# A four-layer-norm attention and feed-forward block: finer first loads, one values step moved ahead of the scores, and a gate on GpSimd's side work

## The chip, the cores and the metric

The kernel runs on one core of a Trainium2 chip. A core has five engines that work side by side, each with its own queue of instructions: TensorE (PE in the profile, with its weight loads as PEld), VectorE (DVE), ScalarE (ACT), GpSimd (POOL) and SyncE (SP), which here only issues DMAs. DMAs are issued from the queues of SP, ACT and POOL. The metric is the device time of one execution in microseconds; the number of a version is the median of its runs.

## The reference

For x of shape 4 x 1024 x 256 (batch, tokens, width), all in float32, the block computes an attention with 16 heads of 16 columns, and a feed-forward with ternary weights, each between two layer norms and with a residual:

```python
def _L0_attn_ref(x, Wqkv, Wout):
    qkv = (x @ Wqkv.T).reshape(B, S, 3, H, Dh)
    qkv = jnp.transpose(qkv, (2, 0, 3, 1, 4))
    q, k, v = (qkv[0], qkv[1], qkv[2])
    scores = jnp.einsum('bhqd,bhkd->bhqk', q, k) * scale
    attn = _stable_softmax(scores)
    out = jnp.einsum('bhqk,bhkd->bhqd', attn, v)
    out = jnp.transpose(out, (0, 2, 1, 3)).reshape(B, S, D)
    return out @ Wout.T
...
h = jax.nn.silu(_tlin(h, w1_w, w1_s)) * _tlin(h, w2_w, w2_s)
h = jax.nn.gelu(_tlin(h, h1_w, h1_s), approximate=False)
h = jax.nn.gelu(_tlin(h, h2_w, h2_s), approximate=False)
return _tlin(h, w3_w, w3_s)
...
x = x + _layernorm(_L0_attn_ref(_layernorm(x, axis=-1), L0_attn_Wqkv, L0_attn_Wout), axis=-1)
x = x + _layernorm(_L0_ffn_ref(_layernorm(x, axis=-1), L0_ffn_w1_w, ...), axis=-1)
```

## The kernel before, in words

**Attention** runs first, for all four batches (b), and takes the first 574 us. It is cut into units: one unit is one batch, one group g of four heads (there are four groups) and one half h of 512 queries. A unit has eight steps c over 128 keys each, and each step has two tiles (u), so 32 units make 512 tiles. For each tile, `exponentials` (lines 547 to 555) multiplies k and q into a score tile `s` of 128 x 1024 in PSUM, and ScalarE writes its exponential into a ring of eight tiles, `e`. `weigh` (557) multiplies the exponentials with the values, which lie in `vaug`, and sums them into the one accumulator `acc`. `rise` (567) keeps a running maximum `top` of the exponentials on VectorE; a ring tile may be written again only when `weigh` and `rise` have read it. `unit_end` (821) transposes the finished accumulator on VectorE (line 824, `o<-acc`), which frees it for the next unit.

The scores are computed from high and low parts of q and k, which must lie in a special order in the tiles `sk` and `sq`. `copies` and `stack` (491 to 526) bring them there by 32 DMA copies for each group (line 500), issued in steps of six: four on SP's queue and two on GpSimd's. Groups 0 and 1 take them from one set of projections, groups 2 and 3 from a second. `slots` (528) copies the values of a group into `vaug` (line 532), on GpSimd except for group 0 of batch 0.

**The main loop** (1464 to 1501) writes the order of all instructions by hand. One round of it makes three score tiles, weighs about as many, and calls `side.take`. `Side` (715) holds chains of `Step`s: a step runs when its `gap` of rounds since the step before it has passed, when `ready()` says so, when TensorE is free of another side step in the round if it needs TensorE, and when its estimated `work` fits. Side chains hold the projections, values and norms of the next batch (`prologue`, 347; `begin`, 789), the ending of the last one (`ending`, 644), the copies of the next stack, and the weight work. The variable `weighed` counts the tiles weighed so far, so `tiles[weighed][3]` is the step c of the unit that is at hand.

**The weight work** on GpSimd prepares the feed-forward's weights. `round_weights` (279) loads a block of `w1`, `w2` or `w3` (line 288), rounds it (292) and stores it (293); six blocks. `round_corners` (299) loads a corner of `h1` or `h2` by two DMAs (309), rounds three quarters of it in two casts (319, 320) and stores them, and then makes four sums and differences (327 to 330) and stores those (312); sixteen corners. The loaded block `w` and the result `wr` have one buffer each, so the sums wait until the store before them has landed. GpSimd also computes the reciprocal roots of all norms (line 107, `rstd`).

**The start** has its own order (1407 to 1454). `load_x(0, [0])` loads x's first 512 tokens on SP's queue, tile 0 by one DMA and tiles 1 to 3 by another (`pieces`, 166), since the halves of the tokens are interleaved; then come the two halves of wqk, with x's second 512 tokens between them. Eight warm-up products on zeros (1413, `idle`) keep TensorE busy meanwhile. VectorE takes statistics of the tiles (97, 98), GpSimd their root, VectorE normalises (140, `xn`), TensorE transposes (381, `pt`), ScalarE copies (342, `xT`), TensorE projects q and k (339, `p`), and the 64 copies of the first stack go out on three queues. Then two of four values steps (`values`, 386; 339, `pv`) run, and the first slots are filled (1448). `alone = False` ends the phase in which side work may use the score tiles' PSUM and ScalarE. The two remaining values steps (1451) are side steps of the first rounds.

**The feed-forward** follows from 574 us on. The change does not touch its code.

Of the kernel before, what the change touches and what calls it, by code (L numbers as in the profile page):

```python
# [73 lines left out]
class Step:  # L74


    def __init__(self, run, gap=0, tensor=True, heavy=False, work=0, split=False):
        self.run, self.gap, self.tensor, self.heavy, self.work, self.split = run, gap, tensor, heavy, work, split
        self.ready = lambda: True


class Norms:
# [61 lines left out]
def tile_fast(ctx: ExitStack, tc: tile.TileContext, x, wqk, wv, wo, w1, w1s, w2, w2s, h1, h1s, h2, h2s, w3, w3s, out, bad):  # L144
    nc = tc.nc
    B, S, D = x.shape
# [3 lines left out]
    NT = S // P  # L150
# [15 lines left out]
    def pieces(h, view):  # L166

        t, n = NH + (TPQ - 1) * h, TPQ * h
        return (slice(n, n + 1), view[:, h : h + 1, :]), (slice(n + 1, n + TPQ), view[:, t : t + TPQ - 1, :])

    def load_x(b, halves=range(NH)):
        view = x[b].rearrange("(t p) d -> p t d", p=P)
        for h in halves:
            for at, tokens in pieces(h, view):
                n = at.stop - at.start
                m = 1 if b == B - 1 else n
                for k in range(0, n, m):
                    nc.sync.dma_start(out=xs[b][:, at.start + k : at.start + k + m, :], in_=tokens[:, k : k + m, :])


    ctx.enter_context(tc.manual_schedule())
    load_x(0, [0])
    ident = const.tile([P, P], F32, name="ident")
    make_identity(nc, ident)
# [28 lines left out]
    with ExitStack() as actx, ExitStack() as rctx:  # L213
# [60 lines left out]
        work = actx.enter_context(tc.tile_pool(name="work", bufs=2, side="right"))  # L274

        def misc(name):
            return ps_misc.tile([P, NQ], F32, tag="misc", name=name)

        def round_weights(n, c):

            st = {}

            def rows(w):
                return w[c * P : (c + rows_at_once[n]) * P, :].rearrange("(i p) d -> p i d", p=P)

            def load():
                st["w"] = work.tile([P, WIDE], F32, tag="w", name="w", bufs=1)
                nc.gpsimd.dma_start(out=st["w"].rearrange("p (i d) -> p i d", i=rows_at_once[n]), in_=rows(weights[n]))

            def cast():  # L290
                st["r"] = work.tile([P, WIDE], F32R, tag="wr", name="wr", bufs=1)
                nc.gpsimd.tensor_copy(st["r"], st["w"])
                nc.gpsimd.dma_start(out=rows(rounded[n]).bitcast(F32), in_=st["r"].bitcast(F32).rearrange("p (i d) -> p i d", i=rows_at_once[n]))

            return [Step(load, 2, False), Step(cast, 4, False)]

        made_factors = [0]

        def round_corners(n, c, x):


            st = {}
            half = NQ // 2

            def load():
                st["w"] = work.tile([P, WIDE], F32, tag="w", name="w", bufs=1)
                rows = weights[n].rearrange("(j c p) (i x n) -> c x p j i n", j=2, p=P, i=2, x=2)[c, x]
                for j in range(2):
                    nc.gpsimd.dma_start(out=st["w"].rearrange("p (j i n) -> p j i n", j=2, i=2)[:, j], in_=rows[:, j])

            def store(r, k0, k1):
                nc.gpsimd.dma_start(
                    out=factors[n][k0:k1, :, c, x * half : (x + 1) * half].rearrange("k p n -> p k n").bitcast(F32),
                    in_=r.bitcast(F32).rearrange("p (k n) -> p k n", n=half)[:, : k1 - k0],
                )

            def plain():
                r = work.tile([P, WIDE], F32R, tag="wr", name="wr", bufs=1)
                nc.gpsimd.tensor_copy(r[:, 0:half], st["w"][:, 0:half])
                nc.gpsimd.tensor_copy(r[:, half : 3 * half], st["w"][:, 2 * half : 4 * half])  # L320
                store(r, 0, 3)

            def sums():
                r = work.tile([P, WIDE], F32R, tag="wr", name="wr", bufs=1)
                s1, s2, s3, s4 = (r[:, k * half : (k + 1) * half] for k in range(4))
                a11, a21, a12, a22 = (st["w"][:, k * half : (k + 1) * half] for k in range(4))
                nc.gpsimd.tensor_tensor(s1, a21, a22, ALU.add)
                nc.gpsimd.tensor_tensor(s2, s1.bitcast(F32), a11, ALU.subtract)
                nc.gpsimd.tensor_tensor(s3, a11, a21, ALU.subtract)
                nc.gpsimd.tensor_tensor(s4, a12, s2.bitcast(F32), ALU.subtract)  # L330
                store(r, 3, 7)
                made_factors[0] += 1

            return [Step(load, 2, False), Step(plain, 3, False), Step(sums, 1, False)]

        def by_slots(o, w, i, **flags):

# [190 lines left out]
        def slots(b, g, t0=0, t1=NT, engine=nc.gpsimd):  # L528


            def run():
                engine.tensor_copy(
                    vaug[g % 2][:, t0:t1, :, 0:DH], cv[:, t0:t1, HPG * DH * g : HPG * DH * (g + 1)].rearrange("p t (h e) -> p t h e", e=DH)
                )
                slotted[g % 2] = b, g, t1

            return run
# [3 lines left out]
        tiles = [(b, g, h, c, u) for b in range(B) for g in range(NG) for h in range(NH) for c in range(NT) for u in range(2)]  # L541
# [173 lines left out]
        class Side:  # L715


            def __init__(self):
                self.first, self.rest, self.slot = [], [], 0
                self.room, self.open, self.tired = 0.0, None, False  # L720
# [58 lines left out]
        side = Side()  # L779
        accs, tops, ends, later = {}, {}, {}, {"qk": 0, "qk1": None}  # L780

        def add_flags(steps):

            if later.setdefault("flags", [[]])[0]:
                later["flags"][0].extend(steps)
            else:
                later["flags"] = side.add(steps)
# [33 lines left out]
        def unit_end(b, g, h):  # L821

            o = both.tile([P, NQ], F32, tag="o", name="o", bufs=2)
            nc.vector.transpose(o, accs[b, g, h])  # L824
            unit = side.add((divide_last if (b, g) == (B - 1, NG - 1) else divide)(g, h, o, tops[b, g, h]), True)
            if b and not g:

                unit[0][-1].ready = lambda: not any(step.tensor for step in ends[b - 1, h][0])
            if g == NG - 1:
                last = ending(b, h, to_scalar if (b, h) == (B - 1, NH - 1) else to_vector)  # L830
                unit[0].extend(last)
                ends[b, h] = unit
            if h < NH - 1:
                return

            n, at = g + 2, b
            if n >= NG:
                n, at = n - NG, b + 1
            if b == B - 1 and g == NG - 2:
                side.add([Step(lambda q=q: load_factor(q), 2 if q else 0, False) for q in range(SLOTS // 2)])  # L840
            if at < B:
                put = Step(slots(at, n), 0, False)
                if at > b:
                    later["chain"][0].append(put)
                else:
                    put.run()
                side.add(stack(at, n))
            if g == NG - 3 and b + 1 < B:
                later["chain"][0].extend(later["rest"])
            elif g == NG - 3:  # L850
                chunks = [(n, [c]) for n in ("w1", "w2") for c in range(DC)]
                loads = [Step(lambda n=n, c=c: load_weights(n, c), 2 if n == "w1" else 1, False) for n, c in chunks]

                loads[0].ready = lambda: not later["flags"][0]
                loads[DC].ready = lambda: not outstanding
                side.add(loads)
                second = prepare(1, to_vector)
                second[-DC].ready = lambda: not outstanding
                side.add([Step(lambda: None, 3, False)] + prepare(0, to_vector) + second)
            if g == NG - 1:  # L860
                begin(b + 1)
# [545 lines left out]
        norm, xt, qk, v, flags = prologue(0, first_space, first_copy)  # L1407
# [39 lines left out]
            step.run()  # L1447
        slots(0, 0, 0, NT // 2, nc.vector)()
        alone = False
        load_x(1)  # L1450
        side.add(v[2:] + [Step(slots(0, 0, NT // 2, NT, nc.vector), 0, False), Step(slots(0, 1), 0, False)] + sum(qk[1], []) + [Step(lambda: later.update(qk1=0, v=0), 0, False), Step(lambda: add_flags(flags[0] + flags[1]), 0, False)])
        begin(0)
        side.add(stack(0, 1) + few(load_rest(), 1))
        side.add([s for k in blocks for s in round_weights(*k)] + [s for k in corners for s in round_corners(*k)])
# [9 lines left out]
        while weighed < len(tiles):  # L1464
            n = end = made
# [3 lines left out]
            if made == len(tiles):  # L1469
                n = made  # L1470
# [8 lines left out]
            while halves and weighed + 2 <= n:  # L1479
                b, g, h, c, _ = tiles[weighed]  # L1480
# [264 lines left out]
```

## Time and profile before

| what | value |
|---|---|
| median of three runs | 1183.34 us |
| the runs | 1180.86, 1184.16, 1183.34 us |
| the profiled execution, its own time | 1187.39 us |
| its span, first to last instruction | 1185.6 us |
| mean granted TensorE clock in it | 0.996 |
| busy: PE, ACT, DVE, POOL | 1150.1, 892.9, 847.0, 301.0 us |
| first exponential, first unit end | 24.18, 49.73 us |
| last unit end | 573.51 us |

A line of the groups gives the source line, engine, operation, output <- inputs, shapes and count, then busy time and mean duration of one, and after the second bar the idle time of the engine just before them and what ended most of it. A timeline line begins with the start and the busy time in us and ends with the idle time before it. A waits line gives total us, times and the longest. A windows line gives, for a stretch of the span, each engine's busy time with its count, the granted TensorE clock (1.00 is full speed), the share of DMA engines busy, and GB/s. Matmuls are pipelined, so a busy TensorE is not one at its peak. A wait for several things is put down to the one that came last by the profile, which can be the wrong one where the engine named had long been done.

### The profile page before, as it was taken

The page shows a single profiled execution, that of the slowest core. Times are in us where ns is not written, and L with a number is a line of the kernel's source. Part 1 is how long each engine was busy: PE and PEld are TensorE (multiplying, and loading weights), DVE is VectorE, ACT ScalarE, POOL GpSimd, SP SyncE. Part 2 cuts the span into 40 slices and gives each one's busy share as a digit, 9 for nine tenths or more (in the row PEclk, how much of TensorE's full clock was granted, in tenths as well). Part 3 has the DMA queues.
Part 4 walks back from the last instruction along what each step waited for, and adds up shares of the span by engine and source line. Part 5 has one row for each costly group of instructions (what it writes and reads, how often), then busy time and mean ns, then how long its engine had stood idle before and what let it go on. Part 6 is the DMA issues. An engine that isn't in the chain of part 4 may idle for free.

```text
span 1185.6 us, 21591 instructions
## 1 busy us (share of the span) xinstructions
PE 1150.1 (97%) x8122; PEld 715.4 (60%) x8122; DVE 847.0 (71%) x1503; ACT 892.9 (75%) x1061; POOL 301.0 (25%) x458
## 2 busy tenths in 40 slices
PE   8999999999999999999999999999999999999996
PEld 3333333334333343333578889888898888988886
DVE  3576578986877876787785756868668686685856
ACT  3899899988998889999467565676756767566664
POOL 6364265674765563220000000000000000000000
PEclk9999999999999999999999999999999999999999
DMA  5865565666646565463304342254622545225421
GB/s 144 221 176 156 142 187 138 185 182 168 164 140 174 153 171 145 100 158 117 108 26 141 119 161 70 91 183 134 196 71 92 176 141 194 73 91 180 138 72 39
DMA packets 78737, 163.68 MB, mean 138 GB/s; under 512 B 14752, under 2 KB 40992, under 8 KB 78624
## 3 DMA queue, kind: packets, MB, share of 16 engines
q1 hardware_dynamic: 62752, 120.05, 34.6%
q0 software_dynamic: 15200, 41.50, 11.8%
q8 instruction: 66, 1.08, 0.4%
q10 hardware_dynamic: 672, 0.66, 0.2%
q14 instruction: 47, 0.39, 0.1%
HBM read 98.71 MB, written 29.88 MB: 108 GB/s over the span
## 4 chain that ended last, share of the span: by engine, by line
PE 77%; ACT 8%; DVE 7%; issue 3%; DMA 2%; SPq 1%; POOL 1%; ACTq 0%; POOLq 0%; DVEq 0%
PE ph L1072 34%; PE acc L562 13%; PE pg L993 9%; PE s L554 8%; ACT e L555 7%; PE pz L1172 5%; PE p L339 3%; PE py L339 2%; PE pv L339 2%; DVE top L574 1%; DVE st L97 1%; SPq L500 1%; PE fpt L936 1%; DMA w<-in_w_dram 1%; DVE xn L140 0%
## 5 line engine op out<-in xcount | busy, mean ns | idle before, releaser
L555 ACT ACTIVATE e<-s 128x1024 f32<-128x1024 f32 x512 | 484.3, 1041 | 44.0 <-PE s L554 36.8
L562 PE MATMUL acc<-e,vaug 128*32 128x512 f32 (+1 forms) x2552 | 255.6, 515 | 1.9 <-DVE o L824 1.8
L107 POOL TENSOR_TENSOR rstd<-ve,minus_half 128x4 f32<-128x4 f32 (+1 forms) x33 | 38.4, 1163 | 679.6 <-DVE ve L105 679.6
L554 PE MATMUL s<-sq,sk 64*128 64x512 f32 x1024 | 187.1, 443 | 18.2 <-ACT e L555 14.6
L554 PEld LDWEIGHTS s<-sq,sk 64*128 64x128 f32 x1024 | 88.1, 185 | 152.6 <-ACT e L555 112.6
L1072 PE MATMUL ph<-hi,sq 128*128 128x512 f32 x448 | 175.7, 392 | 0.0
L1072 PE MATMUL ph<-lo,sq 128*128 128x512 f32 x448 | 174.7, 390 | 0.0
L1072 PE MATMUL ph<-lo,sk 128*128 128x512 f32 x448 | 174.5, 390 | 0.0
L1072 PE MATMUL ph<-hi,sk 128*128 128x512 f32 x448 | 174.4, 389 | 0.0
L574 DVE TENSOR_TENSOR top<-top,e 128x512 f32<-128x512 f32 x192 | 138.8, 723 | 14.2 <-ACT e L555 8.1
L562 PEld LDWEIGHTS acc<-e,vaug 128*32 128x32 f32 x2552 | 66.0, 109 | 122.0 <-issue 107.2
L967 DVE TENSOR_TENSOR lo<-g,hi 128x1024 fp32r<-128x1024 f32 x48 | 58.8, 1224 | 52.4 <-ACT hi L963 52.4
L1072 PEld LDWEIGHTS ph<-lo,sk 128*128 128x128 f32 x448 | 84.2, 188 | 17.5
L1072 PEld LDWEIGHTS ph<-hi,sk 128*128 128x128 f32 x448 | 84.1, 188 | 17.5
L1072 PEld LDWEIGHTS ph<-lo,sq 128*128 128x128 f32 x448 | 84.2, 188 | 17.1
L1072 PEld LDWEIGHTS ph<-hi,sq 128*128 128x128 f32 x448 | 84.1, 188 | 17.1
L1060 ACT ACTIVATE c<-ph,h_scale 128x512 f32<-128x512 f32 x64 | 40.5, 685 | 52.0 <-PE ph L1072 52.0
L995 ACT ACTIVATE sg<-pg,w_scale 128x512 f32<-128x512 f32 x64 | 44.0, 688 | 44.4 <-PE pg L993 38.0
L967 DVE TENSOR_TENSOR lo<-c,hi 128x1024 fp32r<-128x1024 f32 x48 | 58.2, 1220 | 24.2 <-ACT hi L963 24.2
L339 PE MATMUL p<-xT,wqk_sb 128*32 128x512 f32 x512 | 65.7, 593 | 0.5 <-ACT xT L342 0.5
L996 DVE SCALAR_TENSOR_TENSOR g<-pg,w_scale,sg 128x512 f32<-128x512 f32 x64 | 47.8, 748 | 19.9 <-ACT sg L995 19.9
L1172 PE MATMUL pz<-w_sb,lo 128*128 128x256 f32 x256 | 61.6, 283 | 0.0
(199 smaller groups left out, 1848.2 us busy)
## 6 DMA issues: line engine op xcount, KB each, us to landing
sq<-h_f SPq DMA_DIRECT2D x56, 512.0 KB, 4.0
sk<-h_f SPq DMA_DIRECT2D x56, 512.0 KB, 4.7
w<-in_h_dram POOLq DMA_DIRECT2D x32, 256.0 KB, 5.2
h_f<-wr POOLq DMA_DIRECT2D x16, 512.0 KB, 4.0
x<-in_h_dram SPq DMA_DIRECT2D x16, 512.0 KB, 3.5
top_d<-top SPq DMA_DIRECT2D x30, 256.0 KB, 2.6
folded<-top_d SPq DMA_DIRECT2D x30, 256.0 KB, 3.2
h_f<-wr POOLq DMA_DIRECT2D x16, 384.0 KB, 3.6
```

The source lines that it names most:

```text
L339: nc.tensor.matmul(o[j : j + SLOT, :], w[:, j : j + SLOT], i, **flags)
L554: nc.tensor.matmul(s[:, a, :], stacks[1, g % 2, u][r, c * P : (c + 1) * P], stacks[0, g % 2, u][r, h * NQ : (h + 1) * NQ], start=True, sto ...
L555: nc.scalar.activation(pair(k)[:, u], s, AF.Exp)
L562: nc.tensor.matmul(acc[SLOT * i : SLOT * (i + 1), q0:q1], vaug[g % 2][:, c, i, :], pair(k)[:, i // 2, i % 2, q0:q1], start=c == 0 and q0 = ...
L574: nc.vector.tensor_max(top, top if c > 1 else pair(k - 2)[:, :, :, 0:P], pair(k)[:, :, :, 0:P])
L967: nc.vector.tensor_sub(self.lo[i].t, self.raw[i].t, self.hi[i].t.bitcast(F32))
L993: nc.tensor.matmul(p[:, k, :], homes[n][d][:, m * P : (m + 1) * P], half[:, d, :], start=d == j == 0, stop=d == DC - 1 and j == 1)
L995: nc.scalar.activation(sg, p[:, 0, :], AF.Silu, scale=scales["w1"][:, m : m + 1])
L996: nc.vector.scalar_tensor_tensor(x[i, h][c // 2].t[:, c % 2, :], p[:, 1, :], scales["w2"][:, m : m + 1], sg, ALU.mult, ALU.mult)
L1060: nc.scalar.activation(o.t[:, j, :], (o.t if src is None else src)[:, j, :], AF.Gelu, scale=scale[:, m : m + 1])
L1072: nc.tensor.matmul(p[:, j, :], w, half, start=start and c == n == 0, stop=c == HC // 2 - 1 and n == 1, skip_group_check=True,)
L1172: yield c, lambda half=half, c=c, n=n: nc.tensor.matmul(p[:, j, :D], half[:, t * P : (t + 1) * P], homes["w3"][c], start=c == order[0] and ...
```

## The change

There are three edits. First, x's first 512 tokens are loaded by four DMAs of one tile each. Second, the third values step is emitted before the first scores, after `alone = False`, and no longer as a side step. Third, a function `inside(lead, rest)` makes a condition on the step c of the unit at hand, and four kinds of GpSimd steps get it: the rounding of blocks and the casts of corners (c from 0 to 5), the sums of corners (c from 1 to 4), and the slot copies of coming groups (c from 0 to 5), which also become side steps with a gap of 1 where they ran at once. When all tiles are weighed the condition always holds.

```diff
-    def __init__(self, run, gap=0, tensor=True, heavy=False, work=0, split=False):
+    def __init__(self, run, gap=0, tensor=True, heavy=False, work=0, split=False, ready=lambda: True):
...
-        self.ready = lambda: True
+        self.ready = ready
...
-                m = 1 if b == B - 1 else n
+                m = 1 if b == B - 1 or b == h == 0 else n
...
+        def inside(lead, rest):
+            return lambda: weighed == len(tiles) or lead <= tiles[weighed][3] <= NT - rest
...
-            return [Step(load, 2, False), Step(cast, 4, False)]
+            return [Step(load, 2, False), Step(cast, 4, False, ready=inside(0, 3))]
...
-            return [Step(load, 2, False), Step(plain, 3, False), Step(sums, 1, False)]
+            return [Step(load, 2, False), Step(plain, 3, False, ready=inside(0, 3)), Step(sums, 1, False, ready=inside(1, 4))]
...
-                put = Step(slots(at, n), 0, False)
+                put = Step(slots(at, n), 1, False, ready=inside(0, 3))
...
-                    put.run()
+                    side.add([put])
...
         alone = False
+        v[2].run()
         load_x(1)
-        side.add(v[2:] + [Step(slots(0, 0, NT // 2, NT, nc.vector), 0, False), ...
+        side.add(v[3:] + [Step(slots(0, 0, NT // 2, NT, nc.vector), 0, False), ...
```

In the built program TensorE's order changes at the start only: the third values step (16 matmul instructions, which the trace counts as 32) stands before the first scores, and each half projection of the first two units comes one round earlier. VectorE's and ScalarE's orders follow that and are otherwise the same. SP's changes by the loads of x alone. GpSimd has the same instructions in another order from its first slot copy to the end of attention: between its q and k copies and roots, the casts, sums, stores and slot copies stand elsewhere, and the last corner is made during batch 3's second group instead of its first.

## The prediction

> **What bounds the kernel now.** I read the page first, then the windows view, the timeline of the first 60 us, and the waits of TensorE (PE) and ScalarE (ACT). Two lines of the page name the pair that paces attention (24 to 573 us):
>
> ```profile
> L555 ACT ACTIVATE e<-s 128x1024 f32<-128x1024 f32 x512 | 484.3, 1041 | 44.0 <-PE s L554 36.8
> L554 PE MATMUL s<-sq,sk 64*128 64x512 f32 x1024 | 187.1, 443 | 18.2 <-ACT e L555 14.6
> ```
>
> ScalarE's exponentials lose 44.0 us, 36.8 of it to late scores; TensorE loses little to them. So time is won where ScalarE has no scores to work on. The largest such place is the beginning. Timeline of the first 35 us:
>
> ```profile
> 1.55 6.14 PE L1413 MATMUL idle<-e 128*128 128x512 f32 x8 [1.55 <-DVE heads_bf L269]
> 4.86 0.43 DVE L97 BATCH_NORM_STATS2 st<-x 128x6 f32<-128x256 f32 x1 [1.49 <-DMA x<-in_x_dram]
> 8.39 1.73 PE L381 MATMUL pt<-ident,xn 128*128 128x128 f32 x8 [0.69 <-DVE xn L140]
> 19.28 3.64 PE L339 MATMUL pv<-wv_sb,xT 128*32 128x256 f32 x64
> 23.43 0.70 PE L554 MATMUL s<-sq,sk 64*128 64x512 f32 x2 [0.52 <-DMA sq<-cq0hi]
> 25.50 0.93 PE L554 MATMUL s<-sq,sk 64*128 64x512 f32 x4 [1.36 <-ACT e L555]
> 26.36 3.10 PE L339 MATMUL pv<-wv_sb,xT 128*32 128x256 f32 x32
> 30.22 2.85 ACT L555 ACTIVATE e<-s 128x1024 f32<-128x1024 f32 x3 [2.04 <-PE s L554]
> 31.61 1.91 PE L339 MATMUL pv<-wv_sb,xT 128*32 128x256 f32 x32
> 33.99 2.85 ACT L555 ACTIVATE e<-s 128x1024 f32<-128x1024 f32 x3 [0.91 <-PE s L554]
> ```
>
> VectorE waits 1.49 us for x's second transfer. TensorE then waits twice for DMA copies of q and k (0.52 and 1.36; ScalarE had long been done, so the second is the landing of the other stack's q). The third values step takes 3.10 us, the fourth, the same work, 1.91. The windows view says why:
>
> ```profile
> 23.57:26.98 3.41, 2.04 (x18) 1.09 (x22) 0.30 (x1) 1.77 (x3) 3.41 (x8) 1.00 0.55 129
> 26.98:30.40 3.42, 3.42 (x31) 1.71 (x22) 0.69 (x1) 1.38 (x3) 3.40 (x8) 0.50 0.51 120
> ```
>
> (After the window's length, PE's busy time; third from the end, the granted clock.) After 3.41 us in which TensorE worked 2.04, it ran 3.42 us at half clock.
>
> **x in four transfers.** The issue of the first two took 0.40 and 0.42 us on SP's queue. Tile 0 was issued at 0.74 and landed at 2.70, 1.96 later; the three-tile transfer landed at 4.84. Four issues 0.45 apart should land near 2.7, 3.2, 3.6 and 4.1, so the four statistics (0.53 apart) end near 4.9 instead of 6.57: 1.6 us sooner. But the warm-up products hold TensorE to 7.69, so the transposes start there and the first four end near 8.3 instead of 9.70: 1.4. The two issues added put everything behind them on SP's queue 0.9 later: both wqk halves (landed 6.37 and 9.79) and x's second 512 tokens (8.56). The bytes are unchanged and landing there goes by bandwidth (315 to 400 GB/s from 3 to 9 us), so I put x's second half at 0 to 0.8 later, and the chain that follows it (statistics, root, normalisation, first `ck0lo`, q and k copies) 0.6 to 1.2 sooner than now: 0.9. Bounds of the whole edit: 0 if the later half comes 0.8 late and bandwidth is worse than this, 1.4 if it is not late.
>
> **The third values step before the scores.** It moves 32 products, 1.83 us at full clock (half of the 3.64), ahead of the scores. TensorE would finish the first two steps near 22.0, the third near 23.85; the first score is ready near 22.5 and the second near 24.3 (25.2 less 0.9). So the two waits (1.88) are filled with work; the first score is 0.4 late, the first exponential near 24.6 instead of 24.18. From there: three scores, the fourth values step (1.85), three scores, four value products (0.9), half a projection (1.04). The seventh exponential, today at 33.99, comes 5.7 after the first, at 30.3. That is 3.7 sooner; the projections all sit one slot earlier, and the slot that loses its half falls from some 3.3 to ScalarE's 2.85: 0.4 more. Sum for the start: **4.1 us**. Its copy to cv stays on VectorE, idle then (5.60 us until 29.51). The cover is the copies' landing; if the copies land sooner than I think, up to 0.9 of the step is exposed.
>
> About 1.7 of the 4.1 is the half clock (half of 3.42). The Trainium skill, "TensorE: Matmul & The Clock Gate", Part 1, has the clock halved after at least one idle window of about 3.4 us, in a window that runs free of the kernel. By that rule a 1.36 us wait halves nothing and the step would buy 2.4. The row shows the half clock after a window that was 60% busy, so I take 4.1. That the window is free-running is no contradiction: a repeat with another phase might split the gap, as at 372 us, where 1.83 us of idling left the clock at 1.00. The profiled execution (1187.39 us, span 1185.6) is 4.05 above the median of the runs (1183.34), which run from 1180.86 to 1184.16; I subtract from the median and keep 2.4 as the lower end.
>
> **GpSimd's work.** TensorE's and SP's instruction order is the same but for the start; what moves is GpSimd's queue. No instruction is added. Its sums, casts and slot copies are emitted only at tiles of a unit away from its end, so they pass q and k copies in GpSimd's queue, and the norms' roots (L107).
>
> ```profile
> ACT e L555 <- DVE top L574: 5.2, 4, 1.9
> PE s L554 <- DMA sq<-cq1lo: 2.3, 2, 1.8
> ```
>
> The first line (ScalarE's waits) is the price of collisions: at 240.8 (1.69) and 397.9 (1.87) ScalarE waited for VectorE's `top`, which GpSimd's four sums had slowed from 0.69 to as much as 1.22. A third wait (1.17, at 565) has no GpSimd beside it. At most 3.6 goes; but the same sums run elsewhere, two of them still right behind a slot copy at a unit's start. I take half: 1.8. The unit-end waits (PE acc behind DVE o, 1.8 in all) have GpSimd beside them in small part: 0.2.
>
> Against this stands what is now queued ahead of the copies. In GpSimd's new order the tail of the copies for batch 3, group 2 and for batch 2, group 2 reads: total, k, q, two casts and store, q, q, four sums and store, q, q, q. Before, batch 3's came without weight work:
>
> ```profile
> 448.66 0.81 POOL L312 DMA_DIRECT2D h_f<-wr  x1 [0.30 <-POOL wr L320]
> 452.44 0.73 POOL L327 TENSOR_TENSOR wr<-w 128x256 fp32r<-128x256 f32 x1 [1.98 <-DMA h_f<-wr]
> 455.67 0.82 POOL L312 DMA_DIRECT2D h_f<-wr  x1 [0.30 <-POOL wr L330]
> ...
> 495.05 0.57 POOL L432 TENSOR_TENSOR sum<-sum 128x1 bf16<-128x1 f32 x1 [8.70 <-DVE sum L431]
> 497.99 0.96 POOL L500 DMA_DIRECT2D sq<-cq1lo  x2
> ```
>
> The total waits for VectorE until 495.05. Then: k, q to 496.6; two casts (0.4 and 0.65) and 0.3 to 497.9, the store; the sums use the same buffer and wait until it has landed, some 4 us after issue (3.7 at 448.66), to 502; four sums 3.2 to 4.2; 0.3 and 0.8 for the store; the last three q issue at 506.3 to 508 and land 2.5 to 3 later, 509.4 to 511. The scores that need them ran at 508.4, and their exponential followed without a pause. Cost 1.0 to 2.6, and no work covers it: **1.8**. For batch 2, group 2 the copies are already late by 2.3 (the second line above, SP's copies, landing 372.05); GpSimd's would land at 371 to 373: +0.2, between -0.5 and +1. A root at 482.8 falls behind sums and comes 1.2 late with VectorE waiting: 0.3. The slot copy for group 1 now waits for VectorE ahead of two k copies, which land 10 us before their use. Elsewhere the copies land 4.6 us or more ahead today, or lose the sums before their last q (batch 1, group 2). The weights still end near 507, before the feed-forward at 575, so that stage gains and loses nothing.
>
> Sum: -4.1 -1.8 -0.2 +1.8 +0.2 +0.3 = -3.8. Forecast 1183.34 - 3.8 = **1179.5 us**.
>
> **Rivals.** (a) GpSimd's gate does clear VectorE and the late copies are absorbed: -4.1 -3.6 -0.5 = 1175.1. For it: both collisions are in the first 6 us of a unit; against it: 1.8 of late copies. 0.17. (b) The start gives only 2.4, because the half clock isn't in most timed runs, or because x's second half comes late and the warm-up products bind: -2.4 -1.8 -0.2 +2.3 = -2.1, 1181.2. 0.22. (c) Slower: the three q copies behind the sums. Were the store's landing and the sums at their slow ends (4.4 us, 1.2 each), the copies of both late groups would land near 513 and 374.5: 4.4 and 2.5, each with a half-clock stretch after it (1.7), 10.3 in all against 4.1 gained: 1189.5. It decides (slower by 0.3%) from 7.7 us of such stalls on. 0.16. The likeliest, at 1177.5 to 1181.5, has 0.45.
>
> **Numbers.** About 0.3% (3.5 us) is what a measurement of this kernel tells from no change; that line lies at 1179.8, inside the likeliest case. Faster: (a) and three quarters of the likeliest and a little of (b), 0.55; slower 0.17; the rest 0.28. The range reaches from (a) to most of the way to (c).
>
> **What would show it.** In the changed profile: first statistics wait gone, transposes at about 7.7; values steps of 96 products in a row; first exponential near 24.6, seventh near 30.3; clock 1.00 from 20 to 35; waits of ScalarE on `top` below 3.5; a TensorE wait on `sq<-cq1lo` near 504 (508 less the gain). Wrong it would be if half clock shows again at the start, if the first exponential is later than 25.5, or if waits on q copies exceed 5 us.

## The result, and the profile after

The changed kernel takes 1192.29 us (median of six runs, 1188.60 to 1194.24), the kernel before took 1184.52 beside it (six runs, 1180.86 to 1186.72): a ratio of 1.0064, 95% interval 1.0047 to 1.0081. By the ratio it is slower by 7.6 us. The forecast was 1179.5, faster. The profiled execution took 1194.24 us (span 1192.5, mean granted clock 0.992, against 0.996 before). Attention ends at 580.46 us instead of 573.51; the feed-forward takes the same 612 us in both.

The page's two lines of the pair that paces attention (after the second bar: idle time and what ended most of it):

```profile
L560 ACT ACTIVATE e<-s 128x1024 f32<-128x1024 f32 x512 | 485.1, 1041 | 54.1 <-PE s L559 45.5
...
L559 PE MATMUL s<-sq,sk 64*128 64x512 f32 x1024 | 186.3, 444 | 19.4 <-ACT e L560 13.5
```

The work is unchanged (485.1 us against 484.3), but ScalarE now loses 54.1 us instead of 44.0; of the 10.1 more, 8.7 are put down to late scores (45.5 against 36.8). Yet the start, where the forecast put its gain, went better than forecast. The timeline of the first 30 us:

```profile
7.37 1.25 PE L386 MATMUL pt<-ident,xn 128*128 128x128 f32 x8
...
17.88 5.36 PE L344 MATMUL pv<-wv_sb,xT 128*32 128x256 f32 x96
...
23.74 2.86 ACT L560 ACTIVATE e<-s 128x1024 f32<-128x1024 f32 x3 [1.56 <-PE s L559]
...
26.85 5.61 ACT L560 ACTIVATE e<-s 128x1024 f32<-128x1024 f32 x6 [0.25 <-PE s L559]
```

The transposes begin at 7.37 (forecast 7.7), 96 value products run in a row, the first exponential comes at 23.74 (24.6), the seventh at 29.60 (30.3), and no half clock is granted between 20 and 35 us. Unit 0 ends at 44.25 instead of 49.73: 5.5 us sooner than in this one trace of the kernel before. Then the lead is lost. Where, the lengths of the units say (from one end of a unit to the next, us; "second trace" is another execution of the kernel before, from experiment 11):

| unit (batch, group, half) | before | before, second trace | after |
|---|---|---|---|
| 0 (0,0,0), from the first exponential | 25.55 | 24.01 | 20.51 |
| 1 (0,0,1) | 16.20 | 16.83 | 21.09 |
| 2 (0,1,0) | 16.73 | 16.19 | 18.40 |
| 19 (2,1,1) | 18.29 | 16.47 | 20.50 |
| 21 (2,2,1) | 19.28 | 17.81 | 17.95 |
| 27 (3,1,1) | 15.19 | 15.15 | 18.56 |

Two stretches lose: units 1 and 2, and units 19 and 27. They have different causes.

**Units 1 and 2.** The timeline of the changed kernel in unit 1 (SPq is SyncE's queue, the number after the start is the time its issue took):

```profile
50.66 0.81 SPq L599 DMA_DIRECT2D top_d<-top  x1
...
54.76 0.34 SPq L605 DMA_DIRECT2D folded<-top_d  x1
...
58.32 0.75 DVE L609 TENSOR_TENSOR folded<-folded 128x256 f32<-128x256 f32 x2 [2.96 <-DMA folded<-top_d]
...
61.85 4.69 ACT L560 ACTIVATE e<-s 128x1024 f32<-128x1024 f32 x5 [2.50 <-DVE top L579]
...
62.93 0.49 PE L559 MATMUL s<-sq,sk 64*128 64x512 f32 x2 [2.26 <-ACT e L560]
...
66.20 2.79 PE L567 MATMUL acc<-e,vaug 128*32 128x512 f32 x16 [1.83 <-DVE o L829]
...
69.81 1.02 ACT L560 ACTIVATE e<-s 128x1024 f32<-128x1024 f32 x1 [3.27 <-PE s L559]
```

At the end of a unit its maxima (`top`) go to DRAM and come back folded (`divide`, two DMAs on SyncE's queue); this round trip is called the fold here. Unit 0 ended at 44.25, but its `top_d` was issued at 50.66: SyncE was still issuing the copies of the second stack, its last at 49.97. Before, the last was at 49.03 and the unit ended at 49.73, so the fold's first DMA went out at once. Its two lines of the kernel before:

```profile
49.84 0.42 SPq L594 DMA_DIRECT2D top_d<-top  x1
...
61.14 0.74 DVE L604 TENSOR_TENSOR folded<-folded 128x256 f32<-128x256 f32 x2
```

SyncE's queue had come no sooner although the start had: it waited 2.9 us from about 38.7 and went on at 41.55, just after the last transfer of x of batch 1 had landed at 41.53 (before: 38.81 and 38.80). No run tests why the copies stand behind that landing. In all five traces that leave the fold on SyncE's queue its first DMA goes out at 49.8 to 51.5 us, whether unit 0 ends at 44.0 or at 49.7. The folded tile landed at 58.29, the same moment as before (58.17). There VectorE came to it only at 61.14, 3.0 us after the landing; now VectorE, earlier in its work, stood before it for 2.96 us, ScalarE then waited for VectorE's `top`, TensorE for ScalarE, and two windows of half clock followed.

**Units 19 and 27.** Two waits lines of TensorE and ScalarE:

```profile
PE s L559 <- DMA sq<-cq1lo: 5.3, 2, 3.2
```

```profile
ACT e L560 <- DVE top L579: 6.1, 6, 2.5
```

TensorE's wait for q copies, 2.3 us before, is 5.3: 3.16 in unit 19 and 2.10 in unit 27. ScalarE's wait on `top` hasn't fallen (5.2 before): of the two collisions named in the prediction one is gone and 0.56 us of the other is left, but the 2.50 us of unit 1 have come. What stands ahead of the q copies in unit 27 is GpSimd's timeline:

```profile
499.48 0.41 POOL L324 CAST wr<-w 128x256 fp32r<-128x256 f32 x1
...
500.75 0.81 POOL L317 DMA_DIRECT2D h_f<-wr  x1 [0.30 <-POOL wr L325]
...
505.60 1.17 POOL L332 TENSOR_TENSOR wr<-w 128x256 fp32r<-128x256 f32 x1 [3.04 <-DMA h_f<-wr]
...
511.02 0.96 POOL L505 DMA_DIRECT2D sq<-cq1lo  x2
...
513.85 0.92 PE L559 MATMUL s<-sq,sk 64*128 64x512 f32 x2 [2.10 <-DMA sq<-cq1lo]
```

This is the queue that rival (c) described: casts, store, 3.04 us of waiting for the store, four sums, a store, and only then the last q copies.

### The profile page after: what moved, and what is told of

It reads as the page before. It is cut to its first block, busy times and chain, and to the rows that moved or that the text cites. A ratio compares the mean times of both kernels' runs of the same rounds, so it can differ in the third digit from the quotient of the medians.

```text
span 1192.5 us, 21601 instructions
## 1 busy us (share of the span) xinstructions
PE 1151.2 (97%) x8122; PEld 715.7 (60%) x8122; DVE 845.5 (71%) x1503; ACT 893.2 (75%) x1061; POOL 295.5 (25%) x458
## 4 chain that ended last, share of the span: by engine, by line
PE 75%; DVE 8%; ACT 6%; issue 4%; DMA 3%; POOL 2%; SPq 0%; ACTq 0%; DVEq 0%; POOLq 0%
PE ph L1077 33%; PE acc L567 12%; PE pg L998 9%; PE s L559 8%; ACT e L560 5%; PE pz L1177 5%; PE p L344 3%; PE pv L344 2%; PE py L344 2%; DVE top L579 2%; DMA folded<-top_d 1%; DVE st L97 1%; DMA h_f<-wr 1%; DVE lo L972 1%; PE fpt L941 1%
## 5 line engine op out<-in xcount | busy, mean ns | idle before, releaser
L560 ACT ACTIVATE e<-s 128x1024 f32<-128x1024 f32 x512 | 485.1, 1041 | 54.1 <-PE s L559 45.5
L567 PE MATMUL acc<-e,vaug 128*32 128x512 f32 (+1 forms) x2552 | 259.3, 521 | 3.3 <-DVE o L829 3.1
L559 PE MATMUL s<-sq,sk 64*128 64x512 f32 x1024 | 186.3, 444 | 19.4 <-ACT e L560 13.5
L579 DVE TENSOR_TENSOR top<-top,e 128x512 f32<-128x512 f32 x192 | 141.5, 737 | 14.1 <-ACT e L560 7.7
L1077 PEld LDWEIGHTS ph<-lo,sk 128*128 128x128 f32 x448 | 84.1, 188 | 17.5
L1000 ACT ACTIVATE sg<-pg,w_scale 128x512 f32<-128x512 f32 x64 | 44.0, 688 | 44.4 <-PE pg L998 37.9
```

What stands on the lines that cost most here:

```text
L559: nc.tensor.matmul(s[:, a, :], stacks[1, g % 2, u][r, c * P : (c + 1) * P], stacks[0, g % 2, u][r, h * NQ : (h + 1) * NQ], start=True, sto ...
L560: nc.scalar.activation(pair(k)[:, u], s, AF.Exp)
L567: nc.tensor.matmul(acc[SLOT * i : SLOT * (i + 1), q0:q1], vaug[g % 2][:, c, i, :], pair(k)[:, i // 2, i % 2, q0:q1], start=c == 0 and q0 = ...
L579: nc.vector.tensor_max(top, top if c > 1 else pair(k - 2)[:, :, :, 0:P], pair(k)[:, :, :, 0:P])
L1000: nc.scalar.activation(sg, p[:, 0, :], AF.Silu, scale=scales["w1"][:, m : m + 1])
L1077: nc.tensor.matmul(p[:, j, :], w, half, start=start and c == n == 0, stop=c == HC // 2 - 1 and n == 1, skip_group_check=True,)
```

## The experiments

**Theory S** for units 1 and 2: the start's lead runs into SyncE's queue, through the first unit's fold. Its rival **G**: the gate on GpSimd's work did it. **Theory Q** for units 19 and 27: q copies queued behind the sums. Its rival **V**: the casts' or slot copies' new place beside VectorE. Every experiment was timed beside the kernel before; the ratio has its 95% interval.

**1. The start edits alone.**

```diff
-                m = 1 if b == B - 1 else n
+                m = 1 if b == B - 1 or b == h == 0 else n
...
+        v[2].run()
         load_x(1)
-        side.add(v[2:] + ...
+        side.add(v[3:] + ...
```

> The two start edits alone (x in four transfers, third values step before the scores), GpSimd's queue as before. Theory S (SyncE's queue gives the start's gain back): unit 0 ends 5.5 us sooner than before, but the first unit's fold of the maxima goes out behind the second stack's copies and x of batch 1 on SyncE's queue, which do not come sooner; VectorE waits about 3 us for the folded tile, ScalarE about 2.5 for VectorE, and units 1 and 2 take together 5 to 7 us more than before. Total within 2 us of before. Rival G (the gate on GpSimd did that too): units 1 and 2 as long as before, total 4 to 5.5 us faster than before. In both, units 19 and 27 are as before.

1186.32 us beside 1183.83: ratio 1.0022 (1.0015 to 1.0029), slower by 2.5. Unit 0 ends at 44.03, and units 1 and 2 take 23.74 and 18.82. The timeline:

```profile
51.16 0.53 SPq L594 DMA_DIRECT2D top_d<-top  x1
...
59.40 0.75 DVE L604 TENSOR_TENSOR folded<-folded 128x256 f32<-128x256 f32 x2 [4.28 <-DMA folded<-top_d]
```

VectorE waits 4.28 us for the folded tile, with GpSimd's order as before. G falls as the cause of this stretch: two edits that end unit 0 sooner by 3.6 to 5.7 us (the two traces of the kernel before) lose all of it, and more, without the gate.

**2. The gate alone.** `inside` and the four conditions of the diff, on the kernel before.

> The gate on GpSimd's work alone, start as before. Theory S: units 1 and 2 as before (16.2 and 16.7 us); the loss is in units 5, 19 and 27 (1.0, 2.2, 3.4) with q copies that land late behind weight work, less 1.3 and 0.5 won at the two collisions: 4 to 7 us slower than before. Rival G: units 1 and 2 are longer here as well, 9 to 13 us slower than before.

1189.88 beside 1183.83: 1.0052 (1.0037 to 1.0067), 6.0 slower. Units 1 and 2 take 16.69 and 16.26, units 19 and 27 19.97 and 18.18. As S and Q have it: most of the gate's loss is in those two late units (3.5 and 3.0 us more than in the second trace of the kernel before).

**3. The changed kernel with the first unit's fold on GpSimd's queue.** Two DMAs change their queue, TensorE's, VectorE's and ScalarE's orders stay:

```diff
-            nc.sync.dma_start(out=there.rearrange("i k q -> k i q"), ...
+            (nc.sync if divided["made"] else nc.gpsimd).dma_start(out=there.rearrange("i k q -> k i q"), ...
...
-                nc.sync.dma_start(out=folded, in_=there...
+                (nc.sync if mine else nc.gpsimd).dma_start(out=folded, in_=there...
```

> The changed kernel, with the two DMAs of the first unit's fold (maxima to DRAM and back) on GpSimd's queue instead of SyncE's; every other engine's order is unchanged. Theory S: the folded tile has landed before VectorE needs it, its wait of 2.96 us and ScalarE's of 2.50 are gone, units 1 and 2 take 16 to 17 us each, 5 to 6.5 us faster than the changed kernel, so 0 to 3 us slower than before. Rival G: VectorE still loses its time beside GpSimd's slot copy and casts; within 1.5 us of the changed kernel.

1189.11 beside 1183.83: 1.0047 (1.0031 to 1.0063), so 5.3 slower than the kernel before, where the changed kernel is 7.6 slower. Some 2 us are won, less than expected, and the intervals of the two ratios overlap. Units 1 and 2 are 18.01 and 16.19. The cast and its store stand ahead of the fold's second DMA in GpSimd's queue, so it went out at 49.98 and landed at 55.49, and VectorE still waited 0.50. Its trace has also one more half clock at 250 us.

**4. The start edits with the fold on GpSimd's queue, no gate.**

> The two start edits and the fold of the first unit on GpSimd's queue, no gate. Theory S: the start's gain of 5.5 us stays: 4 to 6 us faster than before. Rival G: the same time as the start edits alone (within 1 us of them).

1181.26 beside 1183.83: 0.9975 (0.9966 to 0.9984), 2.6 faster than the kernel before and 5.1 faster than experiment 1, from which it differs by the queue of two DMAs. The timeline:

```profile
44.15 0.78 POOL L594 DMA_DIRECT2D top_d<-top  x1 [6.31 <-DVE top L574]
...
48.42 0.62 POOL L600 DMA_DIRECT2D folded<-top_d  x1
...
55.30 0.74 DVE L604 TENSOR_TENSOR folded<-folded 128x256 f32<-128x256 f32 x2
```

The fold's first DMA goes out when unit 0 ends, and VectorE doesn't wait. This shows S. This version beats both kernels. It gains 2.6 us, though, not the 4 to 6 expected, which leads to experiment 11.

**5. Experiment 3 with the gate lifted from the sums.** `Step(sums, 1, False)` again; casts and slot copies keep the gate.

> The changed kernel with the first unit's fold on GpSimd's queue, and the gate lifted from the corners' sums alone (casts and slot copies keep it). In GpSimd's order the three last q copies of batch 3, group 2 then come with no weight work ahead of them, those of batch 2, group 2 with two casts and a store ahead of the last one only. Theory Q (q copies queued behind the sums make units 19 and 27 late, and half clock follows): those units go back from 20.2 and 18.5 us to about 17 and 15.2, TensorE's wait on sq<-cq1lo falls from 4.8 us to below 2, no half clock near 369 and 505; 5 to 7 us faster than with the fold on GpSimd's queue alone, 1182 to 1184 us. Rival V (it is the casts' or slot copies' new place, beside VectorE's unit ends): units 19 and 27 stay above 18.5 and 17, within 2 us of that kernel.

1182.46 beside 1183.79: 0.9994 (0.9984 to 1.0003), 6.7 faster than experiment 3. Unit 27 is 15.15 and TensorE's wait on `sq<-cq1lo` 1.4 in all; unit 19 came down to 18.66 only, with a half clock. Q holds for unit 27, and for unit 19 in part. In this trace units 1 and 2 take 20.33 and 17.72 although the fold is on GpSimd's queue: its return went out at 50.82 and landed at 58.09, and VectorE waited 2.24. The gated cast and its store stand ahead of it as in experiment 3.

**6. The reverse: experiment 4 with the sums' gate alone.**

> The two start edits, the first unit's fold on GpSimd's queue, and of the gate the sums' part alone (casts and slot copies as in the kernel before). GpSimd's order puts casts, store, sums and store ahead of the last three q copies of batch 2, group 2 and batch 3, group 2, as the whole gate does. Theory Q: units 19 and 27 are 20 and 18.4 us, half clock after each, 5 to 7 us slower than the start edits with the fold moved, 1186 to 1188.5. Rival: the sums alone do little and need the casts' and slot copies' gate beside them: within 2 us of 1181.3.

1188.73 beside 1184.01: 1.0047 (1.0030 to 1.0064), 7.5 slower than experiment 4. The sums' gate by itself is the gate's loss; V falls. Its trace gives more. In unit 27 it has the same wait as the changed kernel, 2.10 us in front of the same scores:

```profile
511.77 0.79 PE L559 MATMUL s<-sq,sk 64*128 64x512 f32 x2 [2.10 <-DMA sq<-cq1lo]
```

but unit 27 takes 16.81, not 18.56. The windows view of both, cut where each trace's clock can change (length, PE's busy time, ..., granted clock); the changed kernel:

```profile
511.34:514.75 3.41, 1.31 (x8) 0.51 (x11) 2.44 (x7) 2.33 (x3) 1.99 (x3) 1.00 0.53 181
514.75:518.16 3.41, 3.41 (x21) 1.22 (x22) 1.69 (x6) 1.02 (x1) 0.00 (x0) 0.50 0.21 64
```

and the start edits with the sums' gate:

```profile
507.39:510.80 3.41, 2.28 (x20) 0.82 (x14) 2.79 (x6) 3.41 (x5) 3.16 (x5) 1.00 0.50 183
510.80:514.21 3.41, 2.44 (x20) 1.08 (x22) 2.81 (x9) 1.80 (x2) 0.46 (x1) 1.00 0.13 30
```

In the first the wait lies in one window, which is 1.31 of 3.41 us busy, and half clock follows; in the second the window's border cuts the wait in two, both windows are two thirds busy, and the clock stays. So, as an estimate from two traces, the wait costs 1.66 us (16.81 less 15.15) and the half clock behind it 1.75 more (18.56 less 16.81; 1.4 and 1.7 by experiments 2 and 3, whose unit 27 takes 18.18 and 18.48).

The kept traces show what the sums' gate moves besides. The four with the sums gated have 19.1 to 20.5 us in unit 19 and 16.8 to 18.6 in unit 27, the ten others 16.4 to 18.7 and 15.1 to 15.2. Two more units are longer in all four: unit 20 (18.1 to 19.1 against 17.3 to 17.5) and unit 26 (19.1 against 18.3 to 18.4). Nothing here tests why.

**7. x in four transfers alone, fold on GpSimd's queue.**

> The kernel before with x's first 512 tokens in four transfers and the first unit's fold on GpSimd's queue; values steps and gate as before. By the prediction's terms x alone is worth 0.9 to 1.5 us, and the waits for q copies with the half clock behind them stay: unit 0 ends 1 to 1.5 us sooner, 1182.3 to 1183 us. Rival: the half clock has no firm tie to those waits and goes as well, 2.5 to 3.5 us.

1184.37 beside 1183.79: 1.0001 (0.9990 to 1.0013), nothing. The first exponential comes at 22.07 and the first wait for q copies is gone, but the second stays (1.51 us for `sq<-cq0lo`), half clock follows, and unit 0 ends at 47.78, where the second trace of the kernel before has 47.60.

**8. The third values step alone, fold on GpSimd's queue.**

> The kernel before with the third values step ahead of the scores and the first unit's fold on GpSimd's queue; x in two transfers, no gate. By the prediction's terms the filled waits, the half clock and the lighter slots are worth 2.8 to 3.2 us, by the gap of 4 us between both edits' 5.5 and x's 1.5 it is 4: unit 0 ends 3 to 4 us sooner, 1180 to 1181 us. Rival: without the sooner x the copies land later and the step is exposed, 1 to 2 us.

1182.34 beside 1183.79: 0.9994 (0.9985 to 1.0002), at most 1.8 us, less than expected. Unit 0 ends at 45.62, 4.1 sooner than in the first trace, and units 1 to 3 give back 3.8: there the second unit's fold comes late (VectorE waits 2.90 us at 74.96), and half clock follows.

**9. Experiment 4 with the slot copies' gate.**

> The two start edits, the first unit's fold on GpSimd's queue, and of the gate the slot copies' part alone (the weight work as in the kernel before). The prediction gave the slot copies' new place 0.2 us at the unit ends and a share of the 1.8 us of collisions, since a slot copy no longer stands right at a unit's start with the sums behind it. Theory: that share is nil, within 1 us of the start edits with the fold on GpSimd's queue (1181.3). Rival: it wins 1 to 2 us, 1179.5 to 1180.3. GpSimd's copies of q for batch 2, group 2 and batch 3, group 2 have no weight work ahead of them but one cast pair, so units 19 and 27 stay near 17 and 15.2 in both.

1183.09 beside 1184.29: 0.9994 (0.9980 to 1.0008); the interval meets that of experiment 4, so its small loss isn't certain. The timeline shows how it can lose:

```profile
59.85 1.05 POOL L297 CAST wr<-w 128x1024 fp32r<-128x1024 f32 x1
59.87 1.06 DVE L586 SCALAR_TENSOR_TENSOR den<-em,o 128x4 f32<-128x4 f32 x1
...
63.96 2.14 PE L567 MATMUL acc<-e,vaug 128*32 128x512 f32 x16 [2.08 <-DVE o L829]
```

With the slot copy put off, the cast comes first and lies beside VectorE's division, whose first step takes 1.06 us instead of 0.17; the unit ends 1.4 later. Here the gate didn't take GpSimd's work away from VectorE, it put it beside other work of VectorE.

**10. Experiment 4 with the loads of x for batches 2 and 3 and of wo four rounds later.**

```diff
-        side.add(stack(0, 1) + few(load_rest(), 1))
+        side.add(stack(0, 1) + [Step(lambda: None, 4, False)] + few(load_rest(), 1))
```

> The two start edits, the first unit's fold on GpSimd's queue, and the loads of x for batches 2 and 3 and of wo four rounds of the loop later, so that no large load shares the DMA engines with the fold's two transfers. Theory S with traffic (in three traces the fold's second transfer took 3.4, 5.5 and 7.3 us from issue to landing, the longer the more of x was under way): the transfer takes below 3 us, unit 1 falls from 17.4 to about 16.3, 0.5 to 1.5 us faster than with the loads where they were. Rival: unit 1 is held by something else (VectorE's statistics and normalisation in it), same time within 0.5 us.

A miss: 1185.57 beside 1184.29, 1.0004 (0.9991 to 1.0017), no gain on the kernel before, where experiment 4 has 2.6. Unit 1 stays at 17.43, and units 2 and 3 take 21.04 and 18.06. The timeline:

```profile
67.62 0.92 SPq L600 DMA_DIRECT2D folded<-top_d  x1
...
76.87 0.75 DVE L604 TENSOR_TENSOR folded<-folded 128x256 f32<-128x256 f32 x2 [5.96 <-DMA folded<-top_d]
```

The loads, issued at 62.4, now meet the second unit's fold: its return landed 9.2 us after issue, and VectorE waited 5.96. What held unit 1 to 17.4 stays open; that a late fold costs time in its unit and the next is seen once more, at another place.

**11. The kernel before once more.**

> The kernel before once more, for a second trace of it. If half clock follows waits only by the phase of a window that runs free of the program, this trace has another set of half-clock stretches than the first (which had one, at 27 to 30.4 us), and its time differs from 1187.4 by some 1.5 us or more for each; if the half clock belongs to the start's waits, it is at 27 us again.

1181.20 us (one run), clock 0.998. It has no half clock in attention at all. Around the same waits at the start (0.46 and 1.42 us):

```profile
23.70:27.11 3.41, 2.14 (x28) 1.28 (x32) 0.00 (x0) 2.32 (x3) 3.41 (x8) 1.00 0.53 117
27.11:30.53 3.42, 3.42 (x48) 1.55 (x42) 0.69 (x1) 2.83 (x4) 2.71 (x6) 1.00 0.63 139
```

2.14 us busy, and the clock stays; in the first trace it was 2.04, and the clock halved. The two executions of one program differ by 6.2 us, in units 0 (1.5), 5 (0.9), 19 (1.8) and 21 (1.5). Against this trace unit 0 ends only 3.4 us sooner in the changed kernel (47.60 to 44.25), not 5.5. The fold was late here already: unit 0 ended at 47.60, its first DMA went out at 50.53, and VectorE waited 0.12 us for the return. So the fold's slack was 3.0 us in one execution of the kernel before and none in the other.

Half clock between 20 and 35 us stands in three of the five traces with the third values step in its old place (the first trace, experiments 7 and 12), and in none of the nine with the step moved.

**12. A control: the kernel before with the fold on GpSimd's queue.**

> A control: the kernel before with the first unit's fold on GpSimd's queue and nothing else. In two traces of the kernel before the folded tile has landed when VectorE comes to it, or 0.12 us later, so Theory S has nothing to win here: within 1 us of before. Rival: GpSimd's queue is better for the fold in any case, and the 2.5 us that the start edits win with it are its own: 1.5 to 3 us faster.

1184.16 beside 1184.01: 1.0001 (0.9990 to 1.0012). The moved fold alone is worth nothing, as S has it; the gain of experiment 4 is the start's.

**The sum.** Start edits with the fold out of the way, -2.6; the fold left on SyncE's queue, +5.1 (experiments 1 and 4); the gate, +6.0: +8.5 against the 7.6 measured, within the intervals.

## Why the prediction was wrong

Two terms of the sum failed: the start's -4.1 measured +2.5, and the gate's five terms (-1.8, -0.2, +1.8, +0.2 and +0.3, together +0.3) measured +6.0.

- **The first step that failed** is to subtract the start's 4.1 us from the end as if a lead at 30 us were a lead at 573. The lead itself came: unit 0 ends at 48.9 on average in the four traces whose start is unchanged, and at 44.4 in the eight with both start edits, 4.5 sooner. But the prediction followed SyncE's queue for 0.9 us of added issues, up to the landing of q and k, and stopped there. The next thing on that queue that an engine waits for, unit 0's fold, goes out near 50 us however early unit 0 ends, and its slack in the kernel before was 3.0 us or none. VectorE waited for it (2.96 us in the changed kernel, 4.28 in experiment 1), half clock followed, and the start's term became +2.5. No rival named it.
- **x in four transfers** came as worked out (transposes 0.3 earlier than forecast), but alone it gains nothing that the timing can tell (experiment 7). **The third values step** filled the waits, and the first exponential came 0.9 sooner than forecast.
- **The half clock at the start**, 1.7 of the 4.1, went as forecast, but not every execution of the kernel before has it (three of five). The prediction said that "a repeat with another phase might split the gap", and took the full price from one trace all the same. Rival (b)'s start term, 2.4, is near what experiment 4 gives (2.6), but by luck: its two reasons, a half clock that most runs lack and a late second half of x, are not what these traces show. In experiment 4 the lead of the start shrinks behind it: unit 1 takes 17.41 us against 16.2 to 16.8 with the third values step in its old place, and what holds it is open.
- **The second step that failed** is the price of the late q copies. They were forecast in their place and order, and the wait in unit 27, 2.10 us, lies within the 1.0 to 2.6 worked out. For batch 3, group 2, 1.8: measured 3.4, of which by the estimate 1.66 is the wait and 1.75 the half clock that the likeliest case left out. For batch 2, group 2, +0.2: unit 19 is 2.2 longer than in the first trace and 4.0 longer than in the second (16.47). The first trace had 1.83 us of waiting there already, and the prediction took that as the kernel's own.
- **The collisions**, -1.8, are not won by a sum that the time shows. The gate alone had 3.2 us of waits on `top`, the two traces of before 5.2 and 4.2. At 240.8 `top` itself was not slowed (0.69), but VectorE's work ahead of it (a copy into `sq` took 1.22). Unit 21, which held one of the two collisions, takes 17.9 us in all four traces with the sums gated; of the ten others three have 17.8 and seven 18.9 to 19.4, on average 18.8. So some 0.8 may be won there, and unit 20 beside it loses as much. The slot copies' part of the gate gave nothing (experiment 9).
- **Rival (c)** had the sign and, for the gate, the mechanism: stalls on q copies, each with half clock. It put its price at 10.3; the gate measured 6.0. It reached 1189.5 by keeping the start's gain; the fold took that.
- Of the marks set in advance, those of the start came true. The wait on `sq<-cq1lo` came in the unit it was forecast for, ScalarE's waits on `top` did not fall below 3.5 (6.1), and one mark against the forecast came true: waits on q copies above 5 us (5.3).

## What to carry to other kernels

A lead won at one place lasts only as long as every queue behind it leads too: follow each queue from the place of the gain to its next transfer that an engine waits for, and note that transfer's slack, in more than one execution. A condition that holds work back moves it in front of whatever is emitted next on that queue, so look up the copies that have no slack before gating. And price a half clock from several executions, not from one.

## What the runs showed of the hardware

The fourteen traces of this study, cut at the 3.41 us grid on which each trace's clock changes, give 2230 windows at full clock between 20 us and the end of the last unit (worked out from TensorE's busy time and the granted clock; some matmul records may be missing). All 14 windows with TensorE less than 54% busy were followed by half clock, 5 of 16 between 54 and 63%, and none of the 2200 above. The Trainium skill ("TensorE: Matmul & The Clock Gate", Part 1) speaks of an idle window that runs free of the kernel; the free phase agrees with experiments 6 and 11, but a window needn't be idle: a single wait of 1.4 to 2.1 us is enough where TensorE has other pauses beside it and the phase puts them in one window.

The same small transfer, the first unit's fold back from DRAM on GpSimd's queue, took 3.4 us from issue to landing in one trace (experiment 4) and 5.5 and 7.3 in others (3 and 5); the second unit's, on SyncE's queue, took 9.2 beside loads of x (10).
